# A two-layer graph kernel with an FFT convolution: small steps given fixed places, complex products joined on one PSUM bank, spectra loaded in 2 KB rows

## The chip, the cores and the metric

The kernel runs on one core of one Trainium2 chip. The metric is the device time of that core in microseconds (us), as a median of several runs. A profile is one further execution, recorded instruction by instruction.

## The reference, cut to what matters

There are 64 graphs of 256 nodes with 256 features, all in float32. Each passes two layers, and each layer ends in a layer norm over `x + layer(x)`.

```python
# layer 0
deg = adj.sum(-1); deg = where(deg != 0, deg, 1); dis = deg ** -0.5
h   = (dis[:, None] * adj * dis[None, :] + alpha * I) @ x
x   = layernorm(x + h @ W.T + b)
# layer 1
h = relu(bn1(conv1x1(x)));  x_conv = relu(bn2(conv17(h)) + x)     # 17 taps along the nodes
s = x @ w_se.T + b_se;      A = exp(-|s_n - s_m|^2) * adj
x_nmp = A @ relu(x @ w_msg.T + b_msg)
r, z, n = gates([x_conv, x_nmp] @ w_ih.T, x @ w_hh.T);  x = layernorm(x + (1 - z) * n + z * x)
```

## The kernel before, in words

**Stages.** The graphs go in four quarters of 16 (`Q`, `NQ`). For each graph `layer0` (L348) and `layer1` (L435) run as generators whose pieces are interleaved by `graphs` (L994): during piece i of `layer1(g)`, the list `PLACES` (L990) says whether a piece of `layer0(g + 2)` or of some other work is traced next. `layer1` ends its convolution part with the forward Fourier transform of the graph's rows (`p_dft`, L486), copied into the tile `V`. When a quarter is complete, `products` (L564) multiplies its spectra with the weight spectra, which are loaded from DRAM as tiles `u` by `load_u` (L535): 23 frequencies, three real products each, in 12 steps. Then `real_transform`, `complex_begin` and `complex_end` (L651, L683, L739) transform back on VectorE (DVE) and send the rows to DRAM (`xc_d`, L734). `gru` (L856) computes the gates of a graph, seven products of three accumulated matmuls (`p_g`, L872), and the last layer norm.

**What overlaps.** While a quarter's spectra are multiplied, the first graphs of the next quarter already run; as `V` is occupied (`M` is the same memory), their transforms go to a second tile `V2` (`AWAY` remembers which), and `copies` (L1100) moves them into `V` once `complex_end` is through. The first 12 graphs of the second quarter run with no gates beside them (`ALONE`); elsewhere pieces of `gru` of the quarter before are mixed in (`others`, `late`, `early`). After the last quarter's products nothing is left but gates: 12 of the third quarter, with `complex_end` between them, then 16 of the last.

**What sets the order.** [...]`tc.issue_after(i)` puts what is traced inside it behind instruction `i` on `i`'s engine. `mark` (L91) records an instruction, and `paced` (L974) releases `RATES` pieces of `complex_end` behind each marked one.

**Lines that the change and the prediction touch.** In `layer0`: row sums on ScalarE (ACT) with `accum_out` (L358), `deg`/`adeg` on DVE (L369, L373), `dis = deg ** -0.5` on GpSimd (POOL, L371), transposes of adj (`p_adjT`, L380), their copy (L381), the diagonal on DVE (`adjT`, L383), scaled x on ACT (L393), `p_hT` (L401) and its copy (L406), `p_out` (L411), its sum on DVE (L416), layer norm (`layernorm`, L319: statistics L326 to L328, `ln_rs` on POOL L329, `ln_mr` L332, two ACT passes L334) and the store of x1 (L422). The two ACT passes are run by `graphs` at piece `APPLIED = 4` of the next graph, behind that graph's `RELU`. In `layer1`: `x1_transposed` (L425: `p_x1T`, copies L432 and L433), `p_conv` (L448) with its evictions L451 and L452, the squared norms on DVE (L456 to L459), `p_msg` (L469) and its relu (L472), `p_dft` (L486, L491), `p_rows` (L499) with copies L501 and L503, `p_dist` (L510), exponentials (L511), the product with adj (L512), `p_nmp` (L519), its copy L523. All these PSUM tiles come from one pool of four banks, `bank` (L82); gates and the first quarter's products use four others. In `products`, the three products of a step have a bank each, in the order t = 1 (real part times u1), 0 (sum of both parts, `ab`, times u0), 2 (imaginary part times u2); one ACT copy (L587) and two DVE operations (L589, L590) follow.

Of the kernel before, what the change touches and what calls it, by code (L numbers as in the profile page):

```python
# [26 lines left out]
def kernel(  # L27
# [291 lines left out]
    def layernorm(y, eps=LN_EPS):  # L319

        chunks = range(y.shape[1])
        st = small.tile([P, NCH, nc.vector.BN_STATS_DIM], F32, name="ln_st")
        mv = small.tile([P, NCH, nc.vector.BN_AGGR_DIM], F32, name="ln_mv")
        rs = small.tile([P, NCH], F32, name="ln_rs")
        for c in chunks:
            nc.vector.bn_stats(st[:, c, :], y[:, c, :])  # L326
            nc.vector.bn_aggr(mv[:, c, :], st[:, c, :])
        nc.vector.tensor_scalar(rs[:, : len(chunks)], mv[:, : len(chunks), 1], eps, None, op0=ALU.add)  # L328
        nc.gpsimd.tensor_tensor(rs[:, : len(chunks)], rs[:, : len(chunks)], neg_half[:, : len(chunks)], op=ALU.pow)  # L329
        yield  # L330
        mr = small.tile([P, NCH], F32, name="ln_mr")
        nc.vector.scalar_tensor_tensor(mr[:, : len(chunks)], mv[:, : len(chunks), 0], -1.0, rs[:, : len(chunks)], op0=ALU.mult, op1=ALU.mult)  # L332
        for c in chunks:
            nc.scalar.activation(  # L334
                y[:, c, :], y[:, c, :], AF.Identity, bias=mr[:, c : c + 1], scale=rs[:, c : c + 1]
            )

# [6 lines left out]
    EVICTED, RELU = {}, {}  # L344
# [3 lines left out]
    def layer0(g):  # L348
# [14 lines left out]
        if g == 1 or g >= Q and g - 2 not in ALONE:  # L363

            with tc.issue_after(X_SCALED[0] if g == 1 else EVICTED[g - 2]):
                degrees()
        else:
            degrees()
# [4 lines left out]
        nc.vector.tensor_scalar(adeg, deg, alpha_t, None, op0=ALU.mult)  # L373

# [7 lines left out]
        for mc in range(NCH):  # L382
            DIAGONAL[g] = nc.vector.scalar_tensor_tensor(  # L383
                adjT[:, mc, 1, :], ident, adeg[:, mc : mc + 1], adjT[:, mc, 2 * mc, :],
                op0=ALU.mult, op1=ALU.add,
            ).ins


        x1 = work.tile([P, NCH, D], F32, name="x1")
        X1[g] = x1  # L390
        with tc.issue_after(copied.ins) if g < 2 else ExitStack():
            for c in range(NCH):
                X_SCALED[g] = nc.scalar.activation(x1[:, c, :], x_t[:, c, :], AF.Copy, scale=dis[:, c : c + 1]).ins  # L393
# [27 lines left out]
        yield from layernorm(x1)  # L421
# [13 lines left out]
    def layer1(g, place):  # L435
# [9 lines left out]
        for c in range(NCH):  # L445
            p = bank("p_conv1")[:, : D + NSE]
            for k in range(DCH):
                nc.tensor.matmul(  # L448
                    p, x1T[:, k, c * P : (c + 1) * P], wc1[:, k, :], start=k == 0, stop=k == DCH - 1
                )  # L450
            nc.scalar.activation(h[:, c, :], p[:, :D], AF.Relu)  # L451
            EVICTED[g] = nc.scalar.copy(cols[:, c, :, :NSE], p[:, D:].unsqueeze(1).to_broadcast([P, 4, NSE])).ins  # L452
# [6 lines left out]
        last = nc.vector.tensor_scalar(  # L459
            cols[:, :, 2:4, NSE], nsq.unsqueeze(2).to_broadcast([P, NCH, 2]), 0.5, None, op0=ALU.mult  # L460
        )
        mark(last)
        mark(last)
# [8 lines left out]
        relu = nc.scalar.activation(msg, p, AF.Relu)  # L472
# [34 lines left out]
        for c in range(NCH):  # L507
            rows = slice(32 * c, 32 * c + 32)
            p = bank("p_dist")[:, :N]
            nc.tensor.matmul(p, dl[rows, c * P : (c + 1) * P], dr[rows, :], start=True, stop=True)  # L510
            nc.scalar.activation(aT[:, c].rearrange("p n q -> p (n q)"), p, AF.Exp, bias=nsq[:, c : c + 1], scale=2.0)  # L511
        mark(nc.vector.tensor_mul(aT, aT, adjT[:, :, 0:3:2, :]))  # L512
        yield
        if g in ALONE:
            x1_transposed(g + 1)
# [7 lines left out]
        nc.scalar.copy(xn[:, 1 : 1 + DCH], p)  # L523
# [11 lines left out]
    def load_u(n, i):  # L535
        u = ustream.tile([P, DCH, D], F32, name="u")
        nc.sync.dma_start(
            u, ud[i][n * GC : (n + 1) * GC].rearrange("c g o -> (c g) o")[:D].rearrange("(k p) o -> p k o", p=P)
        )
        return u  # L540

    def product(p, j, v, u):

        for k in range(DCH):
            nc.tensor.matmul(p[:, j * D : (j + 1) * D], v[:, k, :], u[:, k, :], start=k == 0, stop=k == DCH - 1)  # L545
# [18 lines left out]
    def products(step):  # L564
# [16 lines left out]
        for t, v in ((1, of_pair(V, RE, step)), (0, ab), (2, of_pair(V, IM, step))):  # L581
            q = KBANK[0](f"p_k{t}")
            for j, n in enumerate(PAIRS[step]):
                product(q, j, v[:, j], load_u(n, t))
            p[t] = half(q)[:, :count]
            if t == 0:
                nc.scalar.copy(re, p[0])  # L587
            elif t == 2:
                nc.vector.tensor_add(im, re, p[1])  # L589
                nc.vector.tensor_sub(re, re, p[2])  # L590
            yield
# [214 lines left out]

    def residual(g):
        nc.gpsimd.dma_start(
            CONV[g], x1_d[g // Q][g % Q].rearrange("(c p) d -> p c d", p=P), accum_op=ALU.add
        )  # L810

    def transposed(g):
# [3 lines left out]
        if in_blocks(g):  # L816
            behind(nc.vector.transpose(xcT.rearrange("p k (s r) -> p k s r", r=RB), CONV.pop(g)))
            nc.gpsimd.tensor_tensor(xcT, xcT, inputs[:, 0 : 2 * DCH : 2 * DCH - 1], op=ALU.add)
            nc.gpsimd.memset(inputs[0:1, 0], 1.0)
# [36 lines left out]
    def gru(g):  # L856
# [39 lines left out]
        with tc.issue_after(own):  # L896
            ended()
        load_x1(g)
        p5 = product(S[1], T1)
        mark(nc.vector.tensor_add(quarter(1, 1), quarter(1, 1), p5), 1)  # L900
# [69 lines left out]
    def run(stage):  # L970
        for _ in stage:
            pass
# [17 lines left out]
    PLACES = (("other",), ("layer0",), (), (), ("layer0",), ("other", "layer0"), ())  # L990
    STATS, APPLIED = len(PLACES) - 1, 4
    ENDS = [iter(())]

    def graphs(first, part, others):  # L994


        for i in part:
            load(first + i + 3)
            given = {"layer0": layer0(first + i + 2) if first + i + 2 < B else iter(()), "other": others[i]}
            for piece, _ in enumerate(layer1(first + i, i)):  # L1000
                if piece == APPLIED:
                    with tc.issue_after(RELU[first + i]):
                        run(ENDS.pop())
                    ENDS.append(given["layer0"])
                elif piece == STATS:
                    next(given["layer0"], "end")
                yield
# [92 lines left out]
    def copies(V2):  # L1100

        waiting = list(AWAY)
        AWAY.clear()
        TILES[0] = V
        for i in waiting:
            copy = nc.vector.tensor_copy if i % 2 else nc.scalar.copy
            copy(V[:, :, :, i * GT : (i + 1) * GT], V2[:, :, :, i * GT : (i + 1) * GT])
            yield

    late = nothing()  # L1110
    for q in range(NQ):
        first = (q + 1) * Q
        more = q + 1 < NQ
        end = chain(complex_end(q), copies(V2) if more else iter(()))
# [11 lines left out]
        for step in range(STEPS):  # L1126
# [5 lines left out]
            if q:  # L1132
                run(take(late, (0, 1, 1, 1, 1, 1, 2, 1, 2, 1, 2, 1)[step] if more else step % 2))
# [10 lines left out]
        if more:  # L1144
            run(late)
            run(end)
            if q == 0:
                scope.close()
                gate = ctx.enter_context(tc.tile_pool(name="gate", bufs=2))
            early = gates(q, range(EARLY))  # L1150
            others = [take(early, 5 if q == 0 else 2) for _ in range(Q)]
            run(graphs(first, range(AHEAD, Q), others))
# [62 lines left out]
```

## Time and profile before

| what | value |
|---|---|
| median of 3 runs (lowest, highest) | 2075.72 us (2074.41, 2077.39) |
| the profiled execution | 2079.83 us, of which the span from first to last instruction is 2078.0 us |
| TensorE (PE) matmul busy | 1996.5 us, 96% |
| DVE / ACT / POOL busy | 1395.1 (67%) / 937.4 (45%) / 663.7 us (32%) |
| DMA moved | 298.04 MB, mean 143 GB/s |
| mean granted TensorE clock | 0.991 |

A busy PE is not a PE at its peak: matmuls are pipelined, and their ends are modelled. A line such as "p_hT L401 <- ACT x L393" says that the matmuls of line 401 that write the tile p_hT sat idle until the ACT instruction of line 393 released them. Each float32 matmul instruction appears as two records.

### The profile page before, as it was taken

The numbers are of one execution on the slowest core, as the hardware profiler recorded it, in microseconds if no ns is written. First come the engines' busy times: TensorE is split into PE (matmuls) and PEld (weight loads), VectorE is DVE, ScalarE is ACT, GpSimd is POOL, SyncE is SP. The second block draws the span as 40 slices with busy tenths as digits, with TensorE's granted clock in tenths as the row PEclk, the third lists the DMA queues.
The fourth block names the chain that finished last, engine by engine and source line by source line (L and its number), as shares of the span: only waits on it lengthen the run. The fifth ranks groups of instructions, "written<-read, shape, count | busy, mean of one in ns | idle before, by whom it ended". The sixth has DMA issues, their size and how long they took to land.

```text
span 2078.0 us, 26334 instructions
## 1 busy us (share of the span) xinstructions
PE 1996.5 (96%) x8157; PEld 1444.4 (70%) x8157; DVE 1395.1 (67%) x3241; ACT 937.4 (45%) x2232; POOL 663.7 (32%) x672
## 2 busy tenths in 40 slices
PE   6999999998999999989999999999999999999997
PEld 5888888877677766767777766666777765555554
DVE  5444458776568897753546889774445899977776
ACT  4676644566432234555553223545554123333333
POOL 3444410122432243232322234322332124434443
PEclk9999999999999999999999999999999999999999
DMA  4765657544447644343326664433333754443331
GB/s 122 232 221 184 195 183 226 174 142 146 107 145 216 201 124 125 114 119 109 102 96 184 202 177 123 126 119 104 107 107 114 232 151 128 126 111 99 99 91 52
DMA packets 305288, 298.04 MB, mean 143 GB/s; under 512 B 84192, under 2 KB 283956, under 8 KB 305150
## 3 DMA queue, kind: packets, MB, share of 16 engines
q1 hardware_dynamic: 245198, 200.37, 33.2%
q10 hardware_dynamic: 44480, 67.39, 9.1%
q0 software_dynamic: 15472, 28.61, 6.1%
q8 instruction: 66, 1.08, 0.2%
q14 instruction: 72, 0.59, 0.1%
HBM read 193.19 MB, written 103.06 MB: 143 GB/s over the span
## 4 chain that ended last, share of the span: by engine, by line
PE 48%; DVE 12%; issue 4%; DMA 4%; POOL 3%; ACT 3%; SPq 0%; ACTq 0%; POOLq 0%; DVEq 0%
PE p_g L872 30%; PE p_k L545 7%; PE p_hT L401 3%; PE p_out L411 2%; PE p_nmp L519 2%; DMA u<-ud 2%; POOL sums L843 1%; DVE ln_st L326 1%; PE p_dist L510 1%; PE p_conv L448 1%; DVE VM L733 1%; ACT x L393 1%; POOL dis L371 1%; POOL ln_rs L329 1%; DVE G L927 1%
## 5 line engine op out<-in xcount | busy, mean ns | idle before, releaser
L872 PE MATMUL p_g<-wall,sums 128*128 128x384 f32 x1536 | 536.2, 489 | 5.6 <-DVE G L900 5.5
L872 PEld LDWEIGHTS p_g<-wall,sums 128*128 128x128 f32 x1536 | 284.4, 190 | 193.0 <-issue 12.7
L872 PE MATMUL p_g<-wall,inputs 128*128 128x384 f32 x1152 | 408.1, 490 | 7.2 <-DVE G L890 7.2
L872 PEld LDWEIGHTS p_g<-wall,inputs 128*128 128x128 f32 x1152 | 217.9, 191 | 158.0 <-DVE G L890 14.1
L843 POOL TENSOR_TENSOR sums<-inputs 128x384 f32<-128x384 f32 x128 | 142.7, 1115 | 317.7 <-PE p_g L872 265.6
L329 POOL TENSOR_TENSOR ln_rs<-ln_rs,neg_half 128x2 f32<-128x2 f32 x129 | 95.0, 738 | 400.9 <-DVE ln_rs L328 329.0
L512 DVE TENSOR_TENSOR aT<-aT,adjT 128x512 f32<-128x512 f32 x64 | 47.3, 740 | 229.1 <-ACT aT L511 229.1
L915 ACT ACTIVATE G<-G 128x512 f32<-128x512 f32 x128 | 80.7, 630 | 265.4 <-DVE G L902 154.5
L545 PE MATMUL p_k<-u,VM 128*128 128x256 f32 x736 | 175.3, 381 | 5.0 <-DMA u<-ud 4.9
L545 PEld LDWEIGHTS p_k<-u,VM 128*128 128x128 f32 x736 | 138.7, 190 | 32.4 <-DMA u<-ud 4.2
L401 PE MATMUL p_hT<-adjT,x 128*128 128x256 f32 x512 | 130.8, 400 | 18.0 <-ACT x L393 7.7
L394 POOL TENSOR_TENSOR x_t<-x_t,b_t 128x512 f32<-128x512 f32 x64 | 89.5, 1399 | 158.5 <-issue 92.1
L448 PE MATMUL p_conv<-wc,xn 128*128 128x259 f32 x512 | 125.3, 383 | 6.4 <-ACT xn L432 5.7
L371 POOL TENSOR_TENSOR dis<-deg,neg_half 128x2 f32<-128x2 f32 x64 | 47.5, 743 | 254.1 <-DVE deg L369 251.3
L411 PE MATMUL p_out<-w,hT 128*128 128x256 f32 x512 | 124.6, 387 | 4.1 <-ACT hT L406 3.7
L401 PEld LDWEIGHTS p_hT<-adjT,x 128*128 128x128 f32 x512 | 95.2, 197 | 40.2 <-ACT x L393 10.7
L519 PE MATMUL p_nmp<-aT,msg 128*128 128x256 f32 x512 | 121.6, 380 | 0.2 <-DVE aT L512 0.2
L469 PE MATMUL p_msg<-wmsg,xn 128*128 128x256 f32 x512 | 121.2, 379 | 0.0
L411 PEld LDWEIGHTS p_out<-w,hT 128*128 128x128 f32 x512 | 97.1, 193 | 32.2 <-ACT hT L406 12.8
L486 PE MATMUL p_dft<-fwd,h 128*128 128x240 f32 x512 | 114.4, 366 | 1.9 <-ACT scols L452 1.9
L448 PEld LDWEIGHTS p_conv<-wc,xn 128*128 128x128 f32 x512 | 95.6, 190 | 29.0 <-ACT xn L432 7.5
L843 POOL TENSOR_TENSOR sums<-inputs,sums 128x384 f32<-128x384 f32 x64 | 68.9, 1077 | 133.9 <-PE p_g L872 133.8
(163 smaller groups left out, 3535.7 us busy)
## 6 DMA issues: line engine op xcount, KB each, us to landing
u<-ud SPq DMA_DIRECT2D x284, 256.0 KB
xn_d<-xn ACTq DMA_DIRECT2D x64, 512.0 KB
inputs<-xn_d SPq DMA_DIRECT2D x64, 512.0 KB
ud<-u_set POOLq DMA_DIRECT2D x39, 480.0 KB, 6.2
adj_t<-in_adj_dram SPq DMA_DIRECT2D x64, 256.0 KB
x_t<-in_x_dram SPq DMA_DIRECT2D x64, 256.0 KB
x_d<-x ACTq DMA_DIRECT2D x64, 256.0 KB
xc_d<-VM SPq DMA_DIRECT2D x64, 256.0 KB
```

Source lines behind the costliest of these rows:

```text
L329: nc.gpsimd.tensor_tensor(rs[:, : len(chunks)], rs[:, : len(chunks)], neg_half[:, : len(chunks)], op=ALU.pow)
L394: nc.gpsimd.tensor_tensor(x_t, x_t, b0_t.unsqueeze(1).to_broadcast([P, NCH, D]), op=ALU.add)
L401: nc.tensor.matmul(p[:, k, :], x1[:, mc, k * P : (k + 1) * P], adjT[:, mc, 1 - mc : 3 - mc, :].rearrange("p n q -> p (n q)"), start=mc == ...
L411: nc.tensor.matmul(p[:, c, :], hT[:, k, c * P : (c + 1) * P], w0[:, k, :], start=k == 0, stop=k == DCH - 1)
L448: nc.tensor.matmul(p, x1T[:, k, c * P : (c + 1) * P], wc1[:, k, :], start=k == 0, stop=k == DCH - 1)
L469: nc.tensor.matmul(p[:, c, :], x1T[:, k, c * P : (c + 1) * P], wmsg[:, k, :], start=k == 0, stop=k == DCH - 1)
L486: nc.tensor.matmul(p[:, t0 * FL : t1 * FL], h[:, c, k * P : (k + 1) * P], fwd[:, first : first + t1 - t0, :].rearrange("p t f -> p (t f)") ...
L519: nc.tensor.matmul(p[:, k, :], msg[:, mc, k * P : (k + 1) * P], aT[:, mc].rearrange("p n q -> p (n q)"), start=mc == 0, stop=mc == NCH - 1,)
L545: nc.tensor.matmul(p[:, j * D : (j + 1) * D], v[:, k, :], u[:, k, :], start=k == 0, stop=k == DCH - 1)
L843: nc.gpsimd.tensor_tensor(S[i], x, y, op=op)
L872: nc.tensor.matmul(p[:, : 3 * HD] if k == 0 else p[:, HD:], a[:, k], wall[:, b, k].rearrange("p t d -> p (t d)"), start=first and k == 0, ...
L915: nc.scalar.activation(rz, rz, AF.Tanh, scale=0.5)
```

## The change

1. **Fixed places.** `layer0` of graphs from the third on gets two more stops, after the row sums and after the diagonal. `PLACES` and `APPLIED` change, so that during `layer1(g)`: the layer norm of graph g + 2 (begun in the round before) is applied at piece 1, behind the conv eviction and the squared norm of g; adj of g + 2 is transposed at piece 1; x of g + 2 is scaled at piece 2, behind `RELU[g]`; and the row sums of g + 3 are taken at the end of the round, behind the copy of `p_nmp`. The relu of msg is put behind the applied norm.
2. **x1 of the next graph is transposed before `p_nmp`** in a fixed set of graphs, `EAGER`, in place of `ALONE`.
3. **Copies from `V2` to `V`** are no longer a chain at the end of `complex_end`: `bring` puts so many behind named instructions of the following graphs.
4. **Paced pieces** are released behind the diagonal in place of the squared norm.
5. **Joined products.** The order becomes t = 0, 2, 1. ACT copies the bank of t = 0 aside (into `ab`), then the matmuls of t = 1 accumulate onto that bank, and ACT copies the sum out; one DVE subtraction is left.
6. **2 KB rows.** `u` is loaded as `(p k) o -> p k o`, each partition's two rows in one piece; `h` is written with its channels permuted to match.
7. **No gates beside the last quarter's products** (`step % 2` becomes 0).
8. **In `gru`**, the product `S[1]` and its addition come ahead of the layer norm of the graph before (`ended`), which is put behind both; the residual's DMA on POOL is put behind the last `memset` of `transposed`.

```diff
@@ layernorm @@
-            nc.scalar.activation(
+            op = nc.scalar.activation(
                 y[:, c, :], y[:, c, :], AF.Identity, bias=mr[:, c : c + 1], scale=rs[:, c : c + 1]
             )
+        if normed is not None:
+            normed.append(op.ins)
@@ layer0 @@
-        if g == 1 or g >= Q and g - 2 not in ALONE:
-            with tc.issue_after(X_SCALED[0] if g == 1 else EVICTED[g - 2]):
-                degrees()
-        else:
+        at = X_SCALED[0] if g == 1 else AGGREGATED.get(g - 3)
+        with tc.issue_after(at) if at else ExitStack():
             degrees()
...
+        if g > 1:
+            yield
...
+        mark(diagonal)
+        mark(diagonal)
+        if g > 1:
+            yield
...
-        with tc.issue_after(copied.ins) if g < 2 else ExitStack():
+        with tc.issue_after(copied.ins if g < 2 else RELU[g - 2]):
             for c in range(NCH):
                 X_SCALED[g] = nc.scalar.activation(x1[:, c, :], x_t[:, c, :], AF.Copy, scale=dis[:, c : c + 1]).ins
@@ layer1 @@
-        mark(last)
-        mark(last)
...
-        relu = nc.scalar.activation(msg, p, AF.Relu)
+        with tc.issue_after(NORMED[-1]) if NORMED else ExitStack():
+            relu = nc.scalar.activation(msg, p, AF.Relu)
...
-        yield
-        if g in ALONE:
+        if g in EAGER:
             x1_transposed(g + 1)
+        yield
@@ load_u, product, products @@
-            u, ud[i][n * GC : (n + 1) * GC].rearrange("c g o -> (c g) o")[:D].rearrange("(k p) o -> p k o", p=P)
+            u, ud[i][n * GC : (n + 1) * GC].rearrange("c g o -> (c g) o")[:D].rearrange("(p k) o -> p k o", k=DCH)
...
-        for t, v in ((1, of_pair(V, RE, step)), (0, ab), (2, of_pair(V, IM, step))):
-            q = KBANK[0](f"p_k{t}")
+        for t, v in ((0, ab), (2, of_pair(V, IM, step)), (1, of_pair(V, RE, step))):
+            q = p[0] if t == 1 else KBANK[0](f"p_k{t}")
...
-                nc.scalar.copy(re, p[0])
-            elif t == 2:
-                nc.vector.tensor_add(im, re, p[1])
-                nc.vector.tensor_sub(re, re, p[2])
+                alone = ab.rearrange("p j k q -> p j (k q)")[:, :count]
+                nc.scalar.copy(alone, half(q)[:, :count])
+            elif t == 1:
+                nc.scalar.copy(im, half(q)[:, :count])
+                nc.vector.tensor_sub(re, alone, half(p[2])[:, :count])
@@ gru @@
-        with tc.issue_after(own):
+        p5 = product(S[1], T1)
+        joined = nc.vector.tensor_add(quarter(1, 1), quarter(1, 1), p5)
+        mark(joined, 1)
+        with tc.issue_after(own), tc.issue_after(joined.ins):
             ended()
         load_x1(g)
-        p5 = product(S[1], T1)
-        mark(nc.vector.tensor_add(quarter(1, 1), quarter(1, 1), p5), 1)
@@ graphs @@
-    PLACES = (("other",), ("layer0",), (), (), ("layer0",), ("other", "layer0"), ())
-    STATS, APPLIED = len(PLACES) - 1, 4
+    PLACES = (("other",), ("layer0",), ("layer0",), (), ("layer0",), ("other", "layer0"), ())
+    STATS, APPLIED = len(PLACES) - 1, 1
...
-                    with tc.issue_after(RELU[first + i]):
+                    with tc.issue_after(EVICTED[first + i]), tc.issue_after(SQUARED[first + i]):
                         run(ENDS.pop())
...
                     next(given["layer0"], "end")
+                    next(of_layer0(first + i + 3), "end")
+                if AWAY and TILES[0] is V:
+                    g = first + i
+                    if g >= 2 * Q:
+                        if piece == 5:
+                            bring(g, nc.scalar.copy, 1, EXP[g])
+                    elif piece == 2:
+                        bring(g, nc.vector.tensor_copy, 4, DIAGONAL[g + 2])
+                    elif piece == 5:
+                        bring(g, nc.scalar.copy, 3, EXP[g])
+                        bring(g, nc.vector.tensor_copy, 5, WEIGHED[g])
@@ the quarters @@
-        end = chain(complex_end(q), copies(V2) if more else iter(()))
+        end = complex_end(q)
...
-                run(take(late, (0, 1, 1, 1, 1, 1, 2, 1, 2, 1, 2, 1)[step] if more else step % 2))
+                run(take(late, (0, 1, 1, 1, 1, 1, 2, 1, 2, 1, 2, 1)[step] if more else 0))
```

`EAGER` is `{0, Q - 4, Q - 3, Q - 2, *range(Q, Q + 13), 2 * Q + 5, 2 * Q + 6, 3 * Q + 5, 3 * Q + 6}`.

## The prediction

> **What bounds the kernel now.** I read the page first, then a table by stages, then who waits for whom in the stages with idle time, then groups by form.
>
> ```profile
> span 2078.0 us, 26334 instructions
> PE 1996.5 (96%) x8157; PEld 1444.4 (70%) x8157; DVE 1395.1 (67%) x3241; ACT 937.4 (45%) x2232; POOL 663.7 (32%) x672
> ```
>
> PE is the bound, and the change alters no matmul count. So only PE's idle time, 2078.0 - 1996.5 = 81.5 us, and time at a lower clock can be won. The table by stages (PE, its weight loads, DVE, ACT, POOL, clock, DMA share, GB/s) says where that lies:
>
> ```profile
> 60.00:235.00 175.00, 175.00 (x873) 147.36 (x872) 77.83 (x199) 122.08 (x313) 81.77 (x77) 1.00 0.68 214
> 235.00:285.00 50.00, 46.46 (x229) 38.29 (x228) 26.58 (x83) 30.04 (x85) 14.95 (x15) 1.00 0.47 153
> 380.00:520.00 140.00, 130.27 (x636) 105.85 (x635) 98.48 (x287) 91.49 (x239) 31.97 (x32) 1.00 0.45 144
> 800.00:960.00 160.00, 152.01 (x644) 111.95 (x643) 99.92 (x273) 85.94 (x222) 42.77 (x47) 0.97 0.39 116
> 920.00:960.00 40.00, 37.00 (x153) 28.06 (x152) 13.31 (x49) 22.04 (x63) 14.74 (x18) 0.87 0.31 88
> 960.00:1105.00 145.00, 142.98 (x620) 105.82 (x619) 66.51 (x177) 81.45 (x212) 44.21 (x48) 1.00 0.36 107
> 1300.00:1460.00 160.00, 151.75 (x641) 111.33 (x640) 99.23 (x270) 85.20 (x219) 43.86 (x47) 0.97 0.39 116
> 1460.00:1600.00 140.00, 138.78 (x597) 102.27 (x596) 62.94 (x166) 77.44 (x199) 40.56 (x43) 1.00 0.32 96
> 1600.00:1684.00 84.00, 80.76 (x344) 64.12 (x343) 69.71 (x131) 13.92 (x25) 8.16 (x8) 1.00 0.75 229
> 1684.00:1849.00 165.00, 154.60 (x498) 89.63 (x497) 156.47 (x305) 52.32 (x98) 68.59 (x63) 1.00 0.48 124
> ```
>
> The idle times are the second number less the third: 0 where weight spectra are made (60 to 235), then 3.5, 9.7, 8.0, 2.0, 8.2, 1.2, 3.2 and 10.4 us. At 920 to 960 the clock is 0.87, a loss of 0.13 x 40 = 5.2 us besides; the same stage recurs 502 us later with the same 0.97. In 1684 to 1849 DVE is busy 156.5 of 165 us: there it is the bound. Now the waits of 380 to 520 and of 1680 to 1900:
>
> ```profile
> PE p_dft L486 <- ACT scols L452: 1.9, 1, 1.9
> PE p_out L411 <- ACT hT L406: 1.7, 2, 0.9
> PE p_hT L401 <- DVE adjT L383: 1.3, 3, 0.6
> PE p_hT L401 <- ACT dist_r L503: 1.2, 1, 1.2
> ```
>
> ```profile
> PE p_g L872 <- DVE G L890: 7.0, 6, 1.6
> PE p_g L872 <- DVE G L900: 5.5, 6, 1.7
> ```
>
> The first kind are small late steps of ACT and DVE, one place each. The second kind is DVE behind with gates and `complex_end` together.
>
> **What the Trainium skill says.** "TensorE: Matmul & The Clock Gate", its table of specifications: ScalarE, VectorE and GpSimd take instructions strictly first in, first out, so a step behind a waiting one is late too. The trace agrees: at 926.03 p_rows starts 2.13 us late behind a DVE queue held by `deg` (L369), which waits for row sums on ACT. Same page, Part 1: the clock halves after an idle stretch (it gives some 3.4 us); here a chain of waits of 1.25 (918.27), 2.13 and 1.05 us (927.33) comes ahead of the 0.87. "PSUM — Partial Sum Buffer", The four PSUM rules: a matmul without the first flag adds to what stands in the bank. Its price is in the trace: the gates do that already, at 490 ns (inputs) against 489 (sums), so joining costs PE nothing as such. "DMA: Bandwidth & Descriptors", Why small descriptors are slow: a fixed cost per packet, 3 cycles on one of 32 for 1 KB. In the trace 1 KB packets of `u` take 46 ns at the median and 4 KB ones 159, on a line 84 ns for 2 KB, 9% less per byte.
>
> **Part by part.**
>
> *Fixed places, 235 to 620 and 800 to 1600.* Instructions per graph are the same. One round on ACT behind the conv: the norm's two passes start 0.49 us apart, msg's relu takes 0.50 to the next start, the scaling passes 0.41 and 0.52 (starts at 117.94 to 122.0). After the last p_msg matmul: 0.20 to the relu, then 0.50 + 0.41 + 0.52 = 1.63 us until x is scaled; PE meanwhile has p_dft, 8 records x 202 ns, and p_rows, 2 x 109, = 1.83 us. So p_hT waits 0 to 0.2 us where it now waits 0.38 (the six of 960 to 1080) to 1.97 (887.21); I take 0.08 over some 48 graphs without other cover, 4 us lost, with ends 0 and 10. `deg`, `dis` and the diagonal are then half a round early: the waits on L393, L369 and L383 go. Behind the relu now queue the scaling, L491, L501 and L503: p_dist waits for the last, with p_hT's 1.73 us as cover. The norm's passes, with the x1 store (L422), pass from behind L472 to ahead of it; if `ln_mr` (DVE) is late, the relu and all these are late.
> - 235 to 285: 3.5 idle, waits on L432 (2.1), L406 and L472. x1 is now transposed ahead of p_nmp (8 x 216 ns = 1.73 us), against 0.95 us for the two copies L432 and L433; and the transposes, 4 x 109 ns, stand before p_out, where p_dist alone left 0.2 to 0.9 us. Won: 3.
> - 380 to 520: 9.7 idle. p_out's constant 0.20 us, under the threshold of the list, goes as well. Eight rounds up to 510 took 108.6 us (p_out at 401.40 to 509.98), the best of them 12.33, which holds that 0.20: 108.6 - 8 x 12.13 = 11.5 us. Won: 9. The row sums and L523 stay ahead of the conv eviction; that is the tightest place.
> - 800 to 960 and 1300 to 1460: 8.0 and 8.2 idle; I take 6 of each, and both half clocks (5.2 each; ends 0 and 5.2): 22 together.
> - 960 to 1105, 1460 to 1600, 520 to 620: 1.5 + 1 + 0.5 = 3.
> - Start: 0.7 (x1T to conv) and at best 1.7 (p_u on taps): 1.5.
> The `V2` copies were 24, on ACT 841 ns and on DVE 553 each, at the end of `complex_end`; now 15 on ACT and 9 on DVE, between exponentials and L523, where ACT waits for p_nmp anyway (102.5 us of idle before L523). Nothing; without that cover 3 x 0.84 = 2.5 us a quarter. SP's loads keep their places; adj is needed half a round sooner, with two buffers, after p_adjT two rounds earlier. POOL's residual DMA passes one 0.3 us memset: nothing, as it is 36 times and well ahead of p_xcT.
>
> *Joined products.* DVE loses the addition (L589), ACT gains a copy like L587:
>
> ```profile
> L587 ACT COPY VM<-p_k 128x512 f32<-128x512 f32 x44 | 25.7, 584 | 115.2 <-PE p_k L545 110.4 <-DVE VM L595 4.8
> L589 DVE TENSOR_TENSOR VM<-VM,p_k 128x512 f32<-128x512 f32 x44 | 30.0, 682 | 30.6 <-PE p_k L545 30.6
> ```
>
> With the four small ones that is 31.6 us off DVE and 27.2 on ACT, which is at most half busy there. New on PE's path: the four matmuls of t = 1 wait for the copy, behind it the whole of PE. Cover: the four of t = 2, 8 x 216 = 1.73 us; need 0.20 + 0.58 + 0.1. Slack 0.85 us. I went through the 48 copies of L587: 42 start 0.20 us after the end of t = 0, five at 0.35 to 0.99, one (293.04) at 2.24. So 0.14 + 1.39 = 1.5 us lost; ends 0 and 0.85 a step late. DVE's saving lies in stages without idle PE (620 to 800): 0.
>
> *2 KB rows.* Waits on `u` outside the last quarter, 0.8 + 1.75 us start to start: 1 won. Conv's eviction (L451) reads with stride: L491 does so already at 469 ns for 384 elements, on the line of 381 for 256: nothing.
>
> *Last quarter.* Without gates the products ask 71 loads of 256 KB in 71 x 4 x 216 ns = 61.3 us, 304 GB/s; now 229 GB/s at a share of 0.75, 305 at full, and 9% more with 2 KB. DMA waits (3.2 us of idle) mostly go, SP's queue being free of gate loads. But six pieces of gates, 1.5 graphs, move into a DVE-bound stage whose rate (1.35 pieces per mark) is unchanged; they come after its end, at PE's pace. DVE's sum, not PE's, sets 1684 to 1849, and it falls by 12 x 0.6 = 7 us, while DVE idles more in the first four steps. Taken together: 1 won, ends -5 and +8. The order in `gru` shifts DVE's work, no sum: 0.
>
> *Sum:* 3 + 9 + 22 + 3 + 1.5 + 1 + 1 = 40.5, less 4 and 1.5: 35, say 36 with the small waits I left out. The profiled execution, 2079.8 (span and 1.8 around it), would come to 2044; it lay 4.1 above the median, to which I apply the same 36: **2039.7**.
>
> **Rivals.** (1) *New waits in place of old.* ACT's round has almost no slack; the norms wait for DVE, and 0.4 us a graph over 48 is 19 us: 2059. For: 1.83 against 1.63 us. Against: the waits named are half a round early. (2) *Slower: the joined bank.* In 600 to 800 and 1120 to 1300 DVE is busy 31 to 37 of 40 us, and ACT's gate tanh waits for it; a copy held behind it holds PE. A step gains loss beyond 0.85 us; at a mean of 1 us over 36 steps the gain is gone, at 2.5 late it is 36 x 1.65 = 59: 2099. Against: 46 of the 48 now come in time. (3) *The last products are bound* by DMA or by DVE, 8 us: 2048. (4) *It does nothing:* each wait ends at another instruction at the same time: 2075.
>
> **How the numbers follow.** The forecast 0.60; (1) 0.22; (2) 0.08; (3) 0.06; (4) 0.04. Faster by over 0.2%, which is about what a measurement of this kernel can tell from no change: 0.88; within 0.04; slower 0.08. The unknown ends (half clocks, p_hT, last stage) give the forecast 2014 to 2054; reaching into (1): 2014 to 2064.
>
> **What would show it.** Right: idle PE under 2 us in the stages named, p_conv <- L432 and p_rows <- L369 gone, the clock at 1.00 outside start and end, a round of the second quarter's lone graphs at 12.2 us. Wrong: p_hT <- scaled x in every graph, p_k <- ACT, a clock of 0.87 still, or DVE-bound gates longer by more than they leave the products.

## The result, and the profile after

The changed kernel takes 2072.48 us (median of 12 runs, 2067.12 to 2078.15); the kernel before took 2081.12 in the same runs. The ratio is 0.9968 with a 95% interval of 0.9955 to 0.9981: about 7 us faster by the ratio (the two medians are 8.6 us apart), where 36 were forecast. The profiled execution of after (2077.37 us) lies at the upper end of its runs; against that of before (2079.83) it shows 2.5 us. First the page, the lines that answer to those of before:

```profile
span 2075.6 us, 26338 instructions
...
PE 1993.8 (96%) x8157; PEld 1445.7 (70%) x8157; DVE 1360.7 (66%) x3192; ACT 972.6 (47%) x2283; POOL 663.4 (32%) x672
```

DVE lost 34 us and ACT gained 35. Most of it is the joined products: with them taken back (run 5 below) DVE is busy 1389.3 us and ACT 947.1, so 29 and 26 us are theirs. But PE still idles 81.8 us of the span. To see where, I cut both executions at the same work: "conv 3" is the start of `p_conv` of graph 3, and a round is the time from one graph's `p_conv` to the next. The last column is the best kernel found below (run 11).

| stretch | before, us | after, us | last kernel, us |
|---|---|---|---|
| start to conv of graph 3 | 84.4 | 87.2 | 84.3 |
| conv 3 to 13: weight spectra | 155.6 | **173.1** | 157.1 |
| conv 13 to 18 | 105.9 | 103.4 | 103.4 |
| conv 18 to 20 | 45.3 | **50.9** | 45.7 |
| conv 20 to 29: lone graphs | 123.6 | 111.0 | 111.0 |
| conv 29 to 31: first gates | 66.1 | **73.8** | 69.2 |
| conv 31 to 32: second quarter's products | 173.1 | **178.1** | 173.2 |
| conv 32 to 47 | 338.4 | 330.1 | 329.8 |
| conv 47 to 63 | 497.1 | 488.5 | 490.5 |
| conv 63 to the last products | 12.6 | 12.6 | 12.6 |
| last products to the first copy of the last graph's gates | 452.8 | 443.8 | 442.2 |

Rows won add up to 41.0 us, rows lost to 38.6. The forecast put gains in all the rows won, but only some 1 us in the last, which won 9.0; it saw hardly any of the losses. One execution also shows chance: the rows 18 to 20 and 31 to 32 of after each hold a half clock (a stretch in which the granted clock is 0.5), and without it they take 47.5 to 47.7 us in runs 4, 5, 6 and 7, and 175.3 to 175.9 in runs 1, 3, 4, 9 and 10. The table by stages of after (span, PE, its weight loads, DVE, ACT, POOL, clock, DMA share, GB/s):

```profile
87.00:260.00 173.00, 160.03 (x767) 132.79 (x766) 74.18 (x172) 106.43 (x274) 64.43 (x67) 0.96 0.63 187
...
364.00:415.00 51.00, 48.85 (x222) 40.85 (x221) 28.96 (x68) 22.72 (x57) 4.80 (x5) 0.93 0.54 177
415.00:526.00 111.00, 110.09 (x560) 92.47 (x559) 85.88 (x263) 80.80 (x220) 27.39 (x27) 1.00 0.44 145
526.00:599.00 73.00, 68.35 (x249) 44.62 (x248) 35.19 (x83) 32.03 (x78) 32.12 (x35) 0.98 0.48 121
599.00:778.00 179.00, 175.38 (x673) 124.04 (x672) 130.81 (x253) 57.14 (x113) 49.80 (x46) 0.99 0.58 174
...
1609.00:1671.00 62.00, 60.83 (x278) 51.88 (x277) 50.80 (x100) 13.83 (x25) 1.08 (x1) 1.00 0.87 282
```

The lone graphs, 9.7 us idle before, now idle 0.9. The stage of the weight spectra, which idled 0, now idles 13.0 us. It also runs at clock 0.96, and PE is busy 160.0 us there, 4.7 more than in the same stage before (155.3 of 156 us, from 84 to 240). The waits of PE over the whole span of after:

```profile
PE p_nmp L533 <- DVE aT L524: 13.8, 7, 3.5
PE p_hT L410 <- ACT x L402: 11.8, 15, 1.7
PE p_out L420 <- ACT hT L415: 7.6, 8, 1.3
...
PE p_k L559 <- DMA u<-ud: 4.8, 6, 1.3
PE p_rows L509 <- DVE ln_mr L332: 2.4, 4, 1.3
```

The waits on `xn` (L432) and `deg` (L369) are gone, as forecast; the first line is new and the largest.

**The new wait.** Four times, in every second round, p_nmp waits for `aT`. PE and DVE around the first, in after:

```profile
111.65 1.89 PE L420 MATMUL p_out<-w,hT 128*128 128x256 f32 x8
116.69 3.78 PE L533 MATMUL p_nmp<-aT,msg 128*128 128x256 f32 x8 [3.15 <-DVE aT L524]
```

```profile
105.96 0.61 DVE L387 SCALAR_TENSOR_TENSOR adjT<-ident,adeg,adjT 128x128 f32<-128x128 f32 x2
113.70 2.33 DVE L300 TENSOR_TENSOR taps<-taps,scale 85x1024 f32<-85x1024 f32 x1 [7.13 <-DMA taps<-in_conv2T_dram]
115.96 0.68 DVE L524 TENSOR_TENSOR aT<-aT,adjT 128x512 f32<-128x512 f32 x1
```

`aT` is not slow: it stands on DVE behind the multiplication of the taps of the weight spectra (L300), and that waits 7.13 us for its load. (It also takes 2.33 us in place of 1.22, for a reason given in the last section.) SyncE's queue (SPq) shows why the load is late (start, us on the queue, number):

```profile
98.28 0.84 SPq L291 DMA_DIRECT2D taps<-in_conv2T_dram  x2
101.26 0.39 SPq L110 DMA_DIRECT2D x_t<-in_x_dram  x1
101.69 6.49 SPq L291 DMA_DIRECT2D taps<-in_conv2T_dram  x3
108.22 0.34 SPq L292 DMA_DIRECT2D taps<-in_conv2T_dram  x1
108.60 0.65 SPq L293 DMA_DIRECT2D taps<-in_conv2T_dram  x1
```

Two of seven loads go out, then x_t waits on SP for L425, and five stand behind it. SP's waits for that release from 60 to 240 us, before and after:

```profile
SPq L110 <- DVE x L416: 25.7, 12, 2.8
```

```profile
SPq L110 <- DVE x L425: 37.8, 10, 6.3
```

The order of the loads is that of before, but x_t now goes out at 101.26, when two of three stores of spectra (480 KB each, at 99.62 and 100.70) are already out, and the three next loads take 6.49 us to issue. In a like round of the kernel before x_t went out at 113.40, ahead of the first store (115.06); the three next loads took 1.40 us, and after L300 DVE was idle for 1.47 us until `aT` could start.

### The profile page after: what moved, and what is told of

It is laid out like the page before. It is cut to its first block, busy times and chain, and to the rows that moved or that the text cites. A ratio compares the mean times of both kernels' runs of the same rounds, so it can differ in the third digit from the quotient of the medians.

```text
span 2075.6 us, 26338 instructions
## 1 busy us (share of the span) xinstructions
PE 1993.8 (96%) x8157; PEld 1445.7 (70%) x8157; DVE 1360.7 (66%) x3192; ACT 972.6 (47%) x2283; POOL 663.4 (32%) x672
## 3 DMA queue, kind: packets, MB, share of 16 engines
q8 instruction: 66, 1.08, 0.2%
## 4 chain that ended last, share of the span: by engine, by line
PE 75%; DVE 12%; DMA 5%; ACT 3%; issue 2%; SPq 1%; POOL 1%; ACTq 0%; POOLq 0%; DVEq 0%
PE p_g L893 34%; PE p_k L559 10%; PE p_nmp L533 5%; PE p_hT L410 5%; PE p_out L420 4%; PE p_conv L457 4%; PE p_msg L478 3%; PE p_dft L496 3%; PE p_u L308 2%; PE p_dist L520 2%; PE p_x1T L440 1%; DMA u<-ud 1%; DMA taps<-in_conv2T_dram 1%; DMA inputs<-x_d 1%; PE p_adjT L384 1%
## 5 line engine op out<-in xcount | busy, mean ns | idle before, releaser
L864 POOL TENSOR_TENSOR sums<-inputs 128x384 f32<-128x384 f32 x128 | 141.8, 1108 | 332.3 <-PE p_g L893 309.5
L410 PE MATMUL p_hT<-adjT,x 128*128 128x256 f32 x512 | 128.5, 396 | 13.3 <-ACT x L402 11.8
L334 ACT ACTIVATE x_g<-x_g,ln_mr,ln_rs 128x256 f32<-128x256 f32 x128 | 70.0, 593 | 137.8 <-DVE ln_mr L332 133.5
L533 PEld LDWEIGHTS p_nmp<-aT,msg 128*128 128x128 f32 x512 | 98.9, 194 | 30.7 <-DVE aT L524 16.9
L864 POOL TENSOR_TENSOR sums<-inputs,sums 128x384 f32<-128x384 f32 x64 | 79.0, 1234 | 116.2 <-PE p_g L893 115.7
```

Of the source, the lines that this page charges most:

```text
L410: nc.tensor.matmul(p[:, k, :], x1[:, mc, k * P : (k + 1) * P], adjT[:, mc, 1 - mc : 3 - mc, :].rearrange("p n q -> p (n q)"), start=mc == ...
L533: nc.tensor.matmul(p[:, k, :], msg[:, mc, k * P : (k + 1) * P], aT[:, mc].rearrange("p n q -> p (n q)"), start=mc == 0, stop=mc == NCH - 1,)
L864: nc.gpsimd.tensor_tensor(S[i], x, y, op=op)
```

## The experiments

All were timed beside the kernel before, in three groups of runs; its medians in them were 2078.99, 2076.18 and 2077.99. Each ratio is to that kernel in the same group. After was not timed again in them, so what is called slower or faster than after compares medians of different groups, and 3 us or less of that can't be told from nothing.

**1. The taps product behind aT.**

```diff
-        nc.vector.tensor_mul(tp, tp, scale[:KT]...)
+        with tc.issue_after(WEIGHED[n - 1]) if n - 1 in WEIGHED else ExitStack():
+            nc.vector.tensor_mul(tp, tp, scale[:KT]...)
```

> The changed kernel (2072.5 us) with one edit: the multiplication of the taps (L300) is put behind the product aT of the graph before on DVE. Theory A: the 17.5 us lost between the convs of graphs 3 and 13 come from this product, which waits for its load and holds aT behind it, and from the two half clocks that follow: p_nmp's four waits on aT (13.8 us) and both half clocks (3.4 us each) go, conv of graph 13 starts at about 243 in place of 260.3, the whole takes about 2056. Theory B: the loads of taps themselves are the limit of this stage; then the matmuls p_u wait for the taps 3 us in the same four rounds, and the whole stays at 2069 to 2073.

Measured 2073.69, ratio 0.9978 (0.9966 to 0.9991), conv 3 to 13 in 173.6 us: nothing won. The waits of this stretch:

```profile
PE p_u L309 <- DVE taps L301: 14.0, 9, 1.6
```

Theory A fell in this form: p_nmp's four waits became nine of p_u, the matmul that uses the product. B fell too: the waits are not 3 us in four rounds but up to 1.6 in nine, and DVE waits for no load of taps any more. In one such round the product stands behind `aT` (111.33) and an addition of 3.37 us (111.94), starts at 115.24 and ends too late for p_u. So this place behind `aT` is too late, and ahead of it the load has to be there in time.

**2. The old places in the first rounds.** `layer0`, `layer1` and `graphs` keep the stops and edges of before for rounds 0 to 12 (and `EAGER` lacks graphs 0 and 12), so that every engine's order there is meant to be that of before:

```diff
+    G0 = 13
...
-        if g > 1:
+        if g - 2 >= G0:
             yield
...
-                if piece == APPLIED:
-                    with tc.issue_after(EVICTED[first + i]), tc.issue_after(SQUARED[first + i]):
+                if piece == (APPLIED if g >= G0 else 4):
+                    with tc.issue_after(EVICTED[g] if g >= G0 else RELU[g]), tc.issue_after(SQUARED[g]) if g >= G0 else ExitStack():
```

> The changed kernel with rounds 0 to 12 (the stage in which the weight spectra are made) in the places of the kernel before, on every engine the same order as there; the rest as changed. Theory A: the fixed places cost this stage 17 to 20 us and nothing else does: conv of graph 13 at about 240, no p_nmp wait on aT over 0.5 us before it, clock 1.00 from 40 on, the whole about 2053. Rival (the loss is one of layout, that is of the other parts of the change or of where data lies): conv of graph 13 stays at 255 or later, the whole about 2070.

Measured 2054.39, ratio 0.9891 (0.9871 to 0.9910); conv of graph 13 at 241.1, and of all waits of the stretch one of 1.6 us is left. So the fixed places in this stage are what cost the 18 us (2072.48 less 2054.39).

**3. The taps' loads first.** Which part of the places does it? Here all places stay, and only the order on SP changes:

```diff
+        with tc.issue_after(TAPS_SENT[-1]) if TAPS_SENT else ExitStack():
             nc.sync.dma_start(xin[g], x[g].rearrange("(c p) f -> p c f", p=P))
...
+            if first == 0 and i < NPARTS:
+                load_taps(setup, i + 1)
             load(first + i + 3)
```

> The changed kernel with one edit on SP's queue: all seven loads of taps of a part stand ahead of the load of x_t, which waits for L425 on DVE; the orders on DVE and PE stay those of the changed kernel. Moving the taps product behind aT did not help (p_nmp's waits became nine of p_u on the taps product, 1.72 us each), so the order on DVE is not wrong as such; keeping the early places out of this stage brought back 19 us. Theory A2: the taps product comes too late because five of its seven loads stand behind x_t and so behind two of the three stores of spectra (480 KB each): with this edit they land 3 us or more earlier, p_nmp <- aT falls from 13.8 us to under 2, conv of graph 13 starts at 241 to 246, the whole about 2055. Rival B2: the DMA engines are full in that stretch whatever the order, or the buffer comes free too late; the four waits stay over 2 us each and the whole at 2070 or above.

Measured 2051.92, ratio 0.9887 (0.9868 to 0.9906). SP and DVE of this kernel in the same round:

```profile
96.27 2.65 SPq L293 DMA_DIRECT2D taps<-in_conv2T_dram  x5
98.97 0.33 SPq L294 DMA_DIRECT2D taps<-in_conv2T_dram  x1
100.09 0.65 SPq L295 DMA_DIRECT2D taps<-in_conv2T_dram  x1
100.84 1.61 SPq L112 DMA_DIRECT2D x_t<-in_x_dram  x1
```

```profile
106.68 1.22 DVE L301 TENSOR_TENSOR taps<-taps,scale 85x1024 f32<-85x1024 f32 x1 [1.27 <-issue]
110.93 0.69 DVE L525 TENSOR_TENSOR aT<-aT,adjT 128x512 f32<-128x512 f32 x1 [3.03 <-ACT aT L522]
111.54 3.37 DVE L314 TENSOR_TENSOR u_set<-u_set,u_set 120x1024 f32<-120x1024 f32 x1
```

The product is done at 107.9, 3.03 us before `aT` needs DVE; PE has no wait in the view of this stretch, which takes 153.6 us (156.4 and 157.1 in runs 10 and 11, which have the same edit; 155.6 before). With nothing undone, the order on one queue brings back 19.5 us of this stretch. Together with run 2 this shows the cause: the places moved x_t's release against the stores, and the loads that stood behind x_t on SP's queue came late.

**4. Gates back beside the last products** (`0` becomes `step % 2` again).

> The changed kernel with the six pieces of gates put back beside the last quarter's products. From the first matmul of these products to the last record the changed kernel takes 9 us less than the one before (466.9 against 475.9). Theory A: most of that is this part: about 6 us slower than the changed kernel, 2078.5. Rival (my forecast, 1 us from this part; the rest is the order in gru and the joined products): 2073 to 2074.

Measured 2073.41, ratio 0.9973 (0.9961 to 0.9985). The products take 80.2 us instead of 61.6, and the whole stretch from them 446.8 instead of 443.8: 3.0 in the profile, 0.9 in the medians, which can't be told from my 1. So Theory A's 6 fell.

**5. Three banks** (the loop over t = 1, 0, 2, a bank each, the ACT copy and two DVE operations of before).

> The changed kernel with the complex products as before, three banks and the order t = 1, 0, 2, with the 2 KB rows kept. My forecast: the joined bank loses 1.5 us on PE and DVE's saving of 31.6 us lies where it is not needed: 2071. Rival (the DVE time saved in the last quarter, 12 x 0.6 = 7 us, is what shortens the DVE-bound stretch after it): 2077 to 2079.

Measured 2071.37, ratio 0.9966 (0.9952 to 0.9981), against 0.9968: no difference that can be told. The joined bank's own waits in after are two, 0.7 us each, where 1.5 us lost were forecast. The 29 us of DVE's time are worth nothing that can be told here.

**6. The layer norm first in `gru`.** The edit also takes back the other half of part 8: the residual's DMA no longer stands behind the `memset` (that hunk is left out here).

```diff
...
-        p5 = product(S[1], T1)
-        joined = nc.vector.tensor_add(quarter(1, 1), quarter(1, 1), p5)
-        mark(joined, 1)
-        with tc.issue_after(own), tc.issue_after(joined.ins):
+        with tc.issue_after(own):
             ended()
         load_x1(g)
+        p5 = product(S[1], T1)
+        mark(nc.vector.tensor_add(quarter(1, 1), quarter(1, 1), p5), 1)
```

> The changed kernel with the order in gru as before (the layer norm of the graph before ahead of the product S[1] and its addition; the residual's DMA not held behind the memset). From the first matmul of the last products to the first copy of the last graph's gates the kernel before takes 452.8 us, the changed one 443.8; with the gates back beside the products it took 446.8, with three banks 442.6. Theory A: the order in gru is what the remaining 6 us come from: 450 in that stretch, the whole about 2078. Rival (my forecast: it shifts DVE's work and changes no sum): 444 in that stretch, the whole at 2072, and then the 2 KB rows or the shape of the stage as a whole would have brought them.

Measured 2079.00, ratio 1.0012 (1.0000 to 1.0024): 6.5 us slower than after (9 by the two ratios), as much as the whole change gains. The stretch from the last products takes 451.6 us, 443.8 in after. PE's waits in it, first this kernel, then after:

```profile
PE p_g L892 <- DVE G L910: 7.3, 6, 1.8
PE p_g L892 <- DVE G L920: 5.1, 8, 1.2
```

```profile
PE p_g L893 <- DVE G L911: 6.9, 6, 1.5
PE p_g L893 <- DVE ln_mr L332: 1.1, 1, 1.1
```

The wait on L920, p_g behind the last addition of a graph, is the L900 of before. With the norm of the graph before put behind the addition on DVE, it goes. That the wait is for an addition on DVE points to the norm; no run takes the norm and the residual's DMA apart. My 0 for this part was wrong by 6 to 9 us. But conv 31 to 32 takes 173.3 here, as before, not 175 or more: see run 11.

**7. 1 KB rows** (`(k p) o -> p k o`, `h` in plain order).

> The changed kernel with u loaded in 1 KB rows as before (and h written in its plain order). In the second quarter the products take 111.7 us in the changed kernel and 106.2 before, with two new waits on u of 1.5 us at their start. Theory A: 2 KB rows are a small gain (my forecast 1 us): 2073 to 2075, the last products 61.6 to 64, the two waits still there since they come of the order of loads on SP. Rival: the new layout of the rows costs where it is not alone: then 2070 and the second quarter's products at 107.

Measured 2075.73, ratio 0.9990 (0.9978 to 1.0002), 3 us over after by the medians; the two intervals just overlap. No stage of the profile shows 3 us: the last products take 62.1 us (61.6 in after), both at 282 GB/s, and PE waits 4.8 us in all for `u` in either kernel. What the rows win is 0.5 us where it can be seen, and perhaps up to 3. The price worked out for a 2 KB packet came true: 84 ns at the median in after. Conv 31 to 32 is no shorter with 1 KB rows (177.3), so the rows don't cause the loss there.

**8. The fixed places alone**, from round 13 on, with parts 2 to 4 of the change (`EAGER`, `bring`, the paced pieces), which this run keeps; parts 5 to 8 are as before.

> The kernel before with the fixed places from round 13 on alone (rounds 0 to 12 in the old places; three banks, 1 KB rows, gates beside the last products and the order in gru as before). Theory: what the places win from the conv of graph 13 to the last products is 14 to 17 us (with all other parts changed too it was 16.1 less 2 for other parts); the whole at 2061 to 2064, and the two half clocks at 926 and 1428 are gone. Rival: the gain there needs the other parts (the DVE time saved by the joined products, the order in gru): 2070.

Measured 2063.72, ratio 0.9939 (0.9920 to 0.9957): 14.3 us from the places with these parts, so they need neither the joined products nor the order in `gru`; the half clocks at 926 and 1428 are gone. With the 1, -1, 6.5 and 3 us of runs 4 to 7 this makes 24, about what run 2 won (24.6): the parts add, as far as these medians can tell. No run takes parts 2 to 4 one by one.

**9. Two late rounds.** From 402 and from 531 us on PE of after waits twice in a row, 0.44 + 1.71 and 1.32 + 1.71 us, and in this execution the clock halves. ACT in the first of these rounds:

```profile
402.69 1.09 ACT L334 ACTIVATE x<-x,ln_mr,ln_rs 128x256 f32<-128x256 f32 x2 [0.69 <-DVE ln_mr L332]
403.69 0.57 ACT L482 ACTIVATE msg<-p_msg 128x512 f32<-128x512 f32 x1
...
404.30 0.91 ACT L402 ACTIVATE x<-x_t,dis 128x256 f32<-128x256 f32 x2
```

The new chain is norm, relu, scaling, p_hT, and it starts when `ln_mr` does (402.49), which DVE reaches behind the last steps of the inverse transform. At 532 it stands behind a gates' transpose that waits 3.19 us for its load. On the kernel of run 2, two edits take both out of the way. The first moves the last `complex_begin` behind the next graph's pieces. The second puts the transposes behind the squared norm, and spreads the first gates' pieces differently for it (the last two hunks, one of them in `with_gates`, a helper of the changed kernel that runs the first of them):

```diff
-                run(complex_begin(step))
+                if q or step < STEPS - 1:
+                    run(complex_begin(step))
...
                 run(take(begin, 3))
+                if step == STEPS - 1:
+                    run(complex_begin(step))
...
-            behind(nc.vector.transpose(...))
+            with tc.issue_after(SQUARED[max(SQUARED)]) if g < 2 else ExitStack():
+                behind(nc.vector.transpose(...))
...
-        yield from take(early, 5)
+        yield from take(early, 2)
...
+                others[AHEAD + 1] = chain(iter((0,)), take(early, 8))
```

> The kernel with the old places in rounds 0 to 12 (2054.4) and two more edits: the inverse transform's last steps of the first quarter are traced behind the pieces of the next graph (sq, ln_mr and the diagonal go ahead of them on DVE at 383 us), and the first gates' transposes of the second half of that quarter are put behind the squared norms of graph 29, where they held DVE for 3.2 us on a load at 509 us. Theory: the chains p_rows <- ln_mr, p_hT <- scaled x of 2.5 and 3.2 us in these two rounds shrink to under 1 us each, and the half clock after the second (3.4 us) goes: 2045 to 2050. Rival: both rounds wait for the next thing on ACT instead (scaled x comes last in ACT's round anyway): 2052 to 2055.

Measured 2045.51, ratio 0.9855 (0.9836 to 0.9874): 8.9 less than run 2. Conv 18 to 20 takes 45.7 (47.6 without), conv 29 to 31 67.6 (74.8 without).

**10. Both together**: the taps' loads first, the places kept, these two edits.

> The changed kernel with the taps' loads ahead of x_t, and the two edits in the rounds at 383 and 510 us that brought 8.9 us on the kernel with old places. If the gains add: 2043 (2051.9 less 8.9). If the two rounds' chains have another cause when the places are kept throughout: 2048 or more.

Measured 2042.16, ratio 0.9837 (0.9813 to 0.9861). The gains add, and the clock is full from 32 to 2036 us.

**11. The loads of u.** At the start of the second quarter's products, SP in after:

```profile
623.39 0.34 SPq L810 DMA_DIRECT2D inputs<-xn_d  x1
628.32 0.36 SPq L817 DMA_DIRECT2D x_g<-x_d  x1
628.77 2.80 SPq L551 DMA_DIRECT2D u<-ud  x6
```

and SP's waits there:

```profile
SPq L817 <- DMA out_dram<-x_g: 4.5, 1, 4.5
```

x_g waits for a buffer that the output of an earlier graph still holds: its norm, and so its store, is the one that `gru` now does later. The loads of `u` stand behind x_g. The edit puts the norm first again in the last two gates ahead of each quarter's products:

```diff
+        first_norm = EARLY - 2 <= g % Q < EARLY and g < B - Q
+        if first_norm:
+            with tc.issue_after(own):
+                ended()
+            load_x1(g)
         p5 = product(S[1], T1)
```

> As the kernel with the taps' loads first and the two edits, and in the last two gates ahead of each quarter's products the layer norm of the graph before stands ahead of the product S[1] again. Theory: the norm put later makes the output's store later, the load of x_g waits for the buffer on SP (4.5 us at 623.8 in the changed kernel), and the loads of u for the next products stand behind it: the waits p_k <- u of 1.5 and 1.4 us at the start of the second quarter's products go, and that quarter's products take 107 to 108 us in place of 109 to 112; 2 to 4 us less than the kernel without this edit. Rival: the u loads are late for another reason (the load of xc_g, adj): no difference.

SP in this kernel, to be held against the three lines above:

```profile
594.70 0.34 SPq L811 DMA_DIRECT2D inputs<-xn_d  x1
595.14 0.37 SPq L818 DMA_DIRECT2D x_g<-x_d  x1
597.50 5.52 SPq L552 DMA_DIRECT2D u<-ud  x7
```

Measured 2039.86, ratio 0.9821 (0.9801 to 0.9841), the best of all; both waits are gone, the quarter's products take 106.8 us (109.5 in run 10), conv 31 to 32 173.2 (175.9 in run 10). The 2.3 us of the medians lie within the spread of the runs; the stage shows the edit. One wait of 3.15 us of p_nmp on `aT` is back in this profile, at 129.44: five loads of taps take 7.80 us to issue there (from 112.68), so the edit of run 3 doesn't keep every round safe.

## Why the prediction was wrong

- **"0 where weight spectra are made", "SP's loads keep their places".** This step failed, and with 17.5 us in the profile (18 by run 2) it is over half of the miss of 29 us. I read idle time as what a stage can win and took a stage with none as out of reach, though the change re-places its steps too: this stage was put at 0 with no reason given, and its taps' loads came late behind x_t. Per load the order on SP did stay; what moved is x_t's release and the stores against it. The step named the queue and looked at the order in it, not at what each entry waits for.
- **"If `ln_mr` (DVE) is late, the relu and all these are late."** This mechanism was named and not priced; rival 1 priced it, at 0.4 us in every graph. It came in two rounds only, with other work on DVE ahead of `ln_mr` (the inverse transform, a transpose). In this execution they gave back 5.6 and 7.7 us of the 12.6 won between (forecast: 9, and 0.5 more up to 620), 8.9 by run 9.
- **"The order in `gru` shifts DVE's work, no sum: 0."** Wrong in both directions: 6.5 us are won in all (run 6), 8 in the last stretch alone, and 2.7 lost at the second quarter's products (run 10 against run 11; the 5.0 of the table include a half clock). No sum changes, but PE waited at one place of DVE's order (5.5 us on L900 before), and a wait is a matter of place.
- **800 to 1105 and 1300 to 1600.** Forecast 6 + 5.2 and a share of 3, less a share of the 4 for p_hT: some 11 each; measured 8.3 and 8.6 (conv 32 to 47, 47 to 63). Waits on L432 and L369 and both half clocks went. The term that was too small is p_hT just in time: 3.3 us in four waits between 778 and 1108 alone, and p_out on hT 2.7, which I had not priced; PE still idles 7.8 us there, not under 2. Over the whole span p_hT waits 11.8 us for scaled x, in 15 places (7.7 in 9 before), where all of that wait was to go and 4 us to be left.
- **The reading at 926.03.** The wait of p_rows went, as forecast, but the reason given was wrong: the row sums on ACT were done at 923.44 and `deg` waited for nothing. DVE was held by `ln_mr` (L332), which waited 1.34 us for POOL, and then by `ln_mr` and L459, which took 0.94 and 0.97 us in place of 0.16 and 0.17, each up to the end of an addition on POOL.
- **Right in size:** lone graphs (12.3 us a round against 12.2, idle 0.9); joined products, 1.5 lost against no difference; 2 KB rows, 1 against 0.5 to 3; no gates beside the last products, 1 against 0.9 to 3.0; those products at PE's pace, 61.6 us against 61.3 worked out, at 282 GB/s.
- **Start:** forecast 1.5 won. The kernels' starts take 83.9 to 88.2 us up to conv 3 (84.4 before), the longer ones where the first half clock lasts 10.2 us and not 6.8 or a second one follows: nothing that can be told.
- **Clock:** of the half clocks of before between start and end both are gone, as forecast; five others came, behind the new waits. Half of the time on record at half clock is 18.9 us before and 23.6 after.

That the last kernel stands where I forecast the changed one (2039.86 and 2039.7) is luck, and so is how near the 41.0 us of the rows won come to the forecast: the fixed places won less than forecast from 32 on, and the order in `gru` more. But it tells what the losses were worth: 33 us, taken back by four edits of order.

## What to carry to other kernels

A re-placed schedule has to be costed in every stage that it touches, also in those without idle time: there a step that comes later or earlier has nothing to win and can lose. Look in each queue for entries that wait (a load on its buffer, an operation on its load), and for what stands behind them on the same queue, not only at whether the order is kept. And a part that "changes no sum" is worth what PE waits at the place that it moves.

## What was not expected of the hardware

**DVE and GpSimd exclude each other.** The two additions of the weight spectra, one on each (120 x 1024), start together. In before DVE is first, by 0.45 us at most places, and takes 1.22 us. In after POOL is first by 0.09 us in every second round:

```profile
134.52 2.38 POOL L314 TENSOR_TENSOR u_set<-u_set,u_set 120x1024 f32<-120x1024 f32 x1 [2.36 <-ACT u_set L311]
```

```profile
134.61 3.37 DVE L313 TENSOR_TENSOR u_set<-u_set,u_set 120x1024 f32<-120x1024 f32 x1
```

DVE's then ends 1.08 us after POOL's, about its own time: it waited for all of POOL's. The Trainium skill, "SBUF — State Buffer", section "SBUF: two separate sides", has it: the two share a port pair as an exclusive lock, also for a DVE operation with two SBUF inputs against a GpSimd one that reads SBUF, and who starts first keeps it. The trace agrees, but for one pair of before (65.54), where POOL is recorded as 0.70 us first and DVE still takes 1.22; the profile's spans on POOL are rough. The taps product (L300) has two inputs too: at 113.70 POOL's addition is running (from 112.61, for 2.34 us), and L300 takes 2.33 us and ends 1.08 after it, so some 1.1 us of the wait shown above come from this. In the other rounds it delays L425, and so x_t, by 2.1 us; run 3, where DVE's addition still takes 3.37 us, shows that this costs nothing once no load stands behind x_t. No run took the exclusion away by itself.

**A half clock depends on where a wait falls.** The wait of 3.15 us at 116.69, shown above, is followed by eight records of p_nmp that take 3.78 us. PE at 192.02 in the same execution:

```profile
192.02 1.99 PE L533 MATMUL p_nmp<-aT,msg 128*128 128x256 f32 x8 [3.14 <-DVE aT L524]
```

The same wait, and the clock stays full. The clock's records in the thirteen profiles tell the two apart: all half clocks begin and end on a grid of 3.413 us (to 0.003 us; the last of a program ends with it), so they last 3.4, 6.8 or 10.2 us. The windows of that grid around the two waits, in the columns of the tables by stages:

```profile
112.21:115.62 3.41, 1.33 (x7) 0.82 (x5) 1.92 (x1) 0.32 (x1) 2.71 (x2) 1.00 0.81 234
115.63:119.04 3.41, 2.35 (x6) 1.90 (x7) 3.41 (x7) 0.00 (x0) 0.69 (x2) 0.50 0.72 229
187.31:190.72 3.41, 1.57 (x8) 1.03 (x6) 1.56 (x1) 0.56 (x2) 2.48 (x2) 1.00 0.41 123
190.73:194.13 3.40, 2.11 (x11) 1.85 (x12) 3.40 (x6) 0.08 (x1) 0.93 (x2) 1.00 0.53 145
```

The first wait leaves PE idle for 2.08 us of one window, and the next window runs at half clock. The grid cuts the second wait into 1.84 and 1.29 us, and nothing happens. I counted the windows at full clock from 40 us on in all thirteen profiles. Of 40 with 2.0 us or more of idle PE, all 40 are followed by a half clock; of 18 with 1.75 to 2.0 us, 7; of the other 7552, 4, each with the smaller matmuls of p_u (85x120) in it. The other two waits of after have 2.05 us in one window (half clock) and 1.92 (none). The Trainium skill, "TensorE: Matmul & The Clock Gate", Part 1, has the clock fall after an idle window of some 3.4 us and lets the window run freely. The grid agrees; but here no window had to be idle throughout, 2.0 of 3.41 us were enough. So waits of 3.1 to 3.5 us halve the clock or not by where the grid cuts them, and the grid lies differently in each execution. This fits the spread of the runs: 2067 to 2078 us in after, 2045 to 2047 in run 9, where the long waits are gone. No run moved a wait against the grid by itself, and the idle times rest on ends of matmuls that the profile models: the counts are on record, the rule is inferred from them.
